# Attention steps of one kind in pairs: all full steps of a query tile first, its split steps after

## The chip, the cores and the metric

The kernel runs on one core of one Trainium2 chip. Its time is the device time of one execution in microseconds (us); of several runs the median is given. Shorter is better. A profiled execution is a run of its own, with the hardware profiler on, and it has its own time.

The engines are called as in the profile: PE is the matrix engine (PEld its weight loads), ACT the scalar engine, DVE the vector engine, POOL the general engine that also issues the gathers, SP the queue that issues plain transfers. PSUM is the memory into which PE writes.

## The reference, cut to what matters

A layer of graph attention and a mixture of experts, on 4096 rows of 512 numbers, all float32:

```
x = x + gnn(layernorm(x), adj)
x = x + ffn(layernorm(x))

gnn:  q, k, v = x @ Wq, x @ Wk, x @ Wv           # 8 heads of 64
      scores  = q @ k.T / 8 + 0.01*eye - 1e16*(1 - max(adj, eye))
      out     = softmax(scores) @ v @ Wo          # summed over heads
ffn:  2 of 8 experts a row, each gelu(x @ W1 + b1) @ W2 + b2, weighted
```

The adjacency matrix is sparse, and its first rows and columns are much denser than its last. A query attends only to the keys that its row of the adjacency matrix names.

## The kernel before, in words

Four stages follow each other: projections and lists of keys, attention, routing, experts. The change lies in the second.

**Lists and tiles.** The queries are cut into 32 tiles of 128. For a tile, the first stage makes a list of those keys that at least one of its queries needs, in three classes: needed only by the first 64 queries of the tile, needed by both halves, needed only by the last 64. `ROOM` (line 31) holds for each tile the room of the three classes in units of 128 keys, `(ta, tm, tb)`: (3, 22, 3) for the first tile, (6, 8, 6) for the second, (3, 2, 3) for the last eight.

**Steps.** A tile's work is a row of steps (lines 627 to 638). Each has a width of 128 keys by 128 queries:

- one step of kind `own`: the 128 keys of the tile's own rows, loaded by SP;
- `tm` steps of kind `both`, here called full steps: one gathered tile of 128 keys against all 128 queries;
- `ta` steps of kind `split`: two gathered tiles, one of keys for the first 64 queries and one of keys for the last 64.

There are 270 steps: 32 own, 115 full, 123 split. A gathered tile is 128 rows of 4640 bytes (keys, values and mask words), fetched by one indirect transfer from POOL (line 675); there are 115 + 2 x 123 = 361 of them.

**What a step does.** `turn` (line 694) transposes the gathered keys on PE (four transposes a key tile, line 701), ACT copies them out of PSUM (line 703), DVE unpacks the mask bits (line 713). `scores` (line 727) multiplies keys by queries on PE: a full or own step does it as 64 x 128 pieces of the array, 16 matmul records, a split step as 64 x 64 pieces, 64 records (line 738). ACT takes the exponential (line 745), DVE masks (line 751, or 749 for own). `values` (line 757) multiplies the result by the values, 32 records of 128 x 64 a step (line 766), and adds into the tile's output in PSUM from the first step to the last; the steps of a tile can stand in any order after the first.

**Duos and the order of the work.** Steps are taken in pairs, the duos (lines 642 to 645), which never cross a tile: with an odd number of steps a tile's last duo holds one. The order on every engine is the order in which this loop writes the instructions:

```
        duos = []
        for i in range(NT):
            own = [n for n, st in enumerate(steps) if st["i"] == i]
            duos += [own[k : k + 2] for k in range(0, len(own), 2)]
...
        while n < S or any(k >= n for k in later):
            duo(scores, n + 1)
            duo(values, n)
...
                issue(n + 1 + AHEAD)
            for job in later.pop(n, []):
                job()
            duo(turn, n + 3)
```

So one turn of the loop is: scores of the next duo, values of this one, issue of the gathers of the duo six ahead (`AHEAD` is 5, line 1005), whatever stands in `later`, and the transposes of the duo three ahead. What stands in `later` are a finished tile's end (transposes of line 797, output projection of line 805, residual) and, for each group of four tiles, routing for the experts (lines 831 to 1003: statistics, transposes of line 877, gate matmuls of line 886, ranks, scatters by POOL). These jobs hang on the number of the duo, not on its kinds.

**Buffers.** The pool `kvp` holds 20 key tiles (line 622), taken in turn; a gather waits until `values` has read the tile that was in its buffer. `ps_r` is three buffers of two PSUM banks (line 617), taken in turn by the scores, the transposes and the jobs. There are four buffers each of transposed keys and of exponentials.

Of the kernel before, what the change touches and what calls it, by code (L numbers as in the profile page):

```python
# [72 lines left out]
def fast(tc, dram, flag_d, x, adj, Wks, Wqs, Wvs, Wo, Wg, bg, W1, b1, W2, b2, out):  # L73
    with ExitStack() as ctx:
        _fast(ctx, tc, dram, flag_d, x, adj, Wks, Wqs, Wvs, Wo, Wg, bg, W1, b1, W2, b2, out)


def _fast(ctx, tc, dram, flag_d, x, adj, Wks, Wqs, Wvs, Wo, Wg, bg, W1, b1, W2, b2, out):
# [537 lines left out]
    with ExitStack() as s2:  # L616
# [11 lines left out]
        for i in range(NT):  # L628
            ta, tm, tb = ROOM[i]
            order = [("own", ())]  # L630
            for k in range(max(tm, ta)):
                if k < tm:
                    order.append(("both", (ta + k,)))
                if k < ta:
                    order.append(("split", (k, ta + tm + k)))
            for k, (kind, at) in enumerate(order):
                steps.append(dict(i=i, kind=kind, at=at, k=k, last=k == len(order) - 1,
                                  kv=[], wv=[], kT=[]))
# [1147 lines left out]
```

## Time and profile before

| | |
|---|---|
| median of 3 runs | 2134.53 us (2132.27 to 2135.46) |
| the profiled execution's own time | 2268.75 us |
| its span | 2267.0 us |
| PE busy | 2034.1 us, 90% of the span |
| DVE, ACT, POOL busy | 961.2, 799.3, 604.4 us |
| mean granted PE clock | 0.948 |
| attention in the profiled execution | first scores at 465.8 us, last values at 1605.5 us |
| gathers (line 675) | 361, 1.127 us each on POOL |
| PE instructions | 25404 matmul records, as many weight loads |

The profile is one execution. Its page gives the busy time of each engine, groups of equal instructions (count, busy time, mean length, idle time before them and what ended it), and transfers by queue. The trace behind it can be asked for who waited for whom, for the instructions in order of time, and for busy times by stretches. A wait that is put down to "issue" is one that no semaphore event in the trace ended. "PE" rows are matmul records, and matmuls overlap, so a mean length is longer than the time from one start to the next.

### The profile page before, as it was taken

How to read it: one execution, taken by the hardware profiler on the slowest of the kernel's cores; microseconds unless marked ns; L12 is line 12 of the kernel's file. 1: busy time of each engine (PE TensorE's matmuls, PEld its weight loads, DVE VectorE, ACT ScalarE, POOL GpSimd, SP SyncE). 2: the span in 40 equal slices, each digit the busy share in tenths (PEclk: the TensorE clock that was granted, in tenths of full speed). 3: DMA queues.
4: the chain of work that ended last, by engine and by line, in shares of the span. 5: the costliest groups of instructions: out<-in, count | busy, mean ns of one | idle time of the engine just before them, and what ended most of it. 6: DMA issues, size and time to landing. Idle time of an engine off the chain costs nothing. (4 is left out here: it accounts for less than half of the span.)

```text
span 2267.0 us, 59365 instructions
## 1 busy us (share of the span) xinstructions
PE 2034.1 (90%) x25404; PEld 1349.4 (60%) x25404; DVE 961.2 (42%) x2479; ACT 799.3 (35%) x1166; POOL 604.4 (27%) x712
## 2 busy tenths in 40 slices
PE   9999999989999889889797988979419999999997
PEld 4444444478777778777676876768314444444443
DVE  3665555435444445434444543545332332332322
ACT  3333333155445345344353543535102222222221
POOL 2000000144444434433444433342111112112111
PEclk9999999999999999889898998999759999999999
DMA  9878773487777677767677666675682333333332
GB/s 372 311 242 269 243 259 108 151 331 229 251 243 252 222 248 238 245 222 247 208 260 235 238 199 236 232 235 168 220 301 48 70 70 66 71 69 67 70 68 47
DMA packets 177522, 445.43 MB, mean 196 GB/s; under 512 B 23268, under 2 KB 39652, under 8 KB 176996
## 3 DMA queue, kind: packets, MB, share of 16 engines
q0 software_dynamic: 67360, 249.96, 36.5%
q1 hardware_dynamic: 82228, 141.61, 19.1%
q10 hardware_dynamic: 27664, 49.97, 6.1%
q8 instruction: 205, 3.36, 0.6%
q14 instruction: 65, 0.53, 0.1%
HBM read 367.53 MB, written 73.95 MB: 195 GB/s over the span
## 5 line engine op out<-in xcount | busy, mean ns | idle before, releaser
L675 POOL DMA_INDIRECT kv<-kv_d,idx x361 | 407.0, 1127 | 1026.8 <-issue 471.3
L738 PE MATMUL ps<-q,kT 64*64 64x64 f32 (+1 forms) x10224 | 362.4, 243 | 93.7 <-issue 78.9
L751 DVE SCALAR_TENSOR_TENSOR pr<-t,pr 128x1024 f32<-128x1024 uint16 x238 | 285.4, 1225 | 351.2 <-ACT pr L745 351.1
L738 PEld LDWEIGHTS ps<-q,kT 64*64 64x64 f32 (+1 forms) x10224 | 306.4, 152 | 147.6 <-issue 121.6
L703 ACT COPY kT<-pkT 128x512 f32<-128x512 f32 (+1 forms) x270 | 199.0, 783 | 369.9 <-PE pkT L701 250.0
L766 PE MATMUL o<-kv,pr 128*64 128x65 f32 x8640 | 309.4, 230 | 16.0 <-issue 15.6
L745 ACT ACTIVATE pr<-ps 128x1024 f32<-128x1024 f32 x270 | 271.8, 1025 | 124.9 <-PE ps L738 110.9
L766 PEld LDWEIGHTS o<-kv,pr 128*64 128x64 f32 x8640 | 284.8, 144 | 39.3 <-issue 24.8
L1181 PE MATMUL ph<-w,xT 128*128 x568 | 258.5, 598 | 0.7 <-ACT xT L1171 0.7
L1201 PE MATMUL py_e<-w,hT 128*128 x568 | 255.6, 593 | 0.9 <-DVE hT L1195 0.9
L1215 POOL DMA_INDIRECT out_dram<-y,r x71 | 110.8, 1561 | 474.7 <-ACT y L1214 469.8
L701 PE MATMUL pkT<-ident,kv 128*128 128x128 f32 x1572 | 204.7, 277 | 23.3 <-issue 18.8
L701 PEld LDWEIGHTS pkT<-ident,kv 128*128 128x128 f32 x1572 | 174.8, 142 | 48.5 <-issue 38.3
L1181 PEld LDWEIGHTS ph<-w,xT 128*128 128x128 f32 x568 | 103.5, 192 | 104.7 <-issue 103.5
L1201 PEld LDWEIGHTS py_e<-w,hT 128*128 128x128 f32 x568 | 102.5, 190 | 103.5 <-issue 102.3
L1186 DVE TENSOR_TENSOR h<-ph,bb 128x512 f32<-128x512 f32 x71 | 49.1, 692 | 212.8 <-PE ph L1181 209.8
L1213 DVE TENSOR_TENSOR y<-py_e,bb 128x512 f32<-128x512 f32 x71 | 49.1, 692 | 194.2 <-PE py_e L1201 194.2
L591 PE MATMUL pv<-wv,xT 128*128 128x512 f32 x256 | 131.3, 608 | 0.0
L591 PE MATMUL pk<-wk,xT 128*128 128x512 f32 x256 | 128.8, 614 | 0.7 <-ACT xT L389 0.7
L1187 ACT ACTIVATE h<-h 128x512 f32<-128x512 f32 x71 | 44.7, 629 | 233.1 <-DVE h L1186 233.1
L576 PE MATMUL pq<-xT,wq 128*128 128x512 f32 x256 | 125.9, 607 | 0.0
L805 PE MATMUL py<-wo,oT 128*128 128x512 f32 x256 | 121.7, 619 | 0.3 <-ACT pr L745 0.3
(248 smaller groups left out, 1727.2 us busy)
## 6 DMA issues: line engine op xcount, KB each, us to landing
adj<-in_adj_dram SPq DMA_DIRECT2D x64, 1024.0 KB
r<-xs_d SPq DMA_DIRECT2D x71, 258.0 KB
kv_d<-kvr ACTq DMA_DIRECT2D x32, 516.0 KB
kv<-kv_d SPq DMA_DIRECT2D x32, 516.0 KB
w<-in_L_ffn_W_dram ACTq DMA_DIRECT2D x16, 1024.0 KB
xt<-in_x_dram SPq DMA_DIRECT2D x32, 256.0 KB
q_d<-qT ACTq DMA_DIRECT2D x32, 256.0 KB
q<-q_d SPq DMA_DIRECT2D x32, 256.0 KB
```

Of the source, the lines that this page charges most:

```text
L576: nc.tensor.matmul(pq, w["q"][:, c, ts(p, P)], xTs[b][:, c, :], start=(c == 0), stop=(c == DC - 1),)
L591: nc.tensor.matmul(pk, xTs[b][:, c, ts(t, P)], w[n][:, c, :], start=(c == 0), stop=(c == DC - 1),)
L675: nc.gpsimd.indirect_dma_start(out=g, out_offset=None, in_=kv_d, in_offset=bass.IndirectOffsetOnAxis(ap=idx[i // GL][:, i % GL, a : a + 1] ...
L701: nc.tensor.transpose(pk[:, x * NP + p, :], g[:, ts(p, P)], ident)
L703: nc.scalar.copy(kT[:, : nk * NP], pk[:, : nk * NP])
L738: nc.tensor.matmul(ps[c : c + nk, r, p * P + x * nq : p * P + (x + 1) * nq], kT[r * KD : (r + 1) * KD, p, c : c + nk], q[r * KD : (r + 1) ...
L745: nc.scalar.activation(pr.rearrange("p h q -> p (h q)"), ps.rearrange("p r f -> p (r f)"), AF.Exp)
L751: nc.vector.scalar_tensor_tensor(pr, st["t"].unsqueeze(1).to_broadcast([P, H, P]), 0.0, pr, op0=ALU.is_gt, op1=ALU.mult,)
L766: nc.tensor.matmul(o[c * HALF : (c + 1) * HALF, h // NP, (h % NP) * VW : (h % NP + 1) * VW], pr[:, hd * NP + p, c * HALF : (c + 1) * HALF] ...
L805: nc.tensor.matmul(hold["py"], hold["oT"][:, c, :], wo[:, c, :], start=(c == 0), stop=(c == NP - 1),)
L1181: nc.tensor.matmul(ph, xTs[b][:, c, :], w1[:, bass.ds(es[b], 1), c, :], start=(c == 0), stop=(c == DC - 1),)
L1201: nc.tensor.matmul(py, hTs[b][:, c, :], w2[:, bass.ds(es[b], 1), c, :], start=(c == 0), stop=(c == HC - 1),)
```

## The change

Within a tile the order of the steps after `own` changes. Before, full and split steps alternate until one kind runs out; after, all full steps come first and then all split steps. Nothing else is edited.

```
         for i in range(NT):
             ta, tm, tb = ROOM[i]
             order = [("own", ())]
-            for k in range(max(tm, ta)):
-                if k < tm:
-                    order.append(("both", (ta + k,)))
-                if k < ta:
-                    order.append(("split", (k, ta + tm + k)))
+            order += [("both", (ta + k,)) for k in range(tm)]
+            order += [("split", (k, ta + tm + k)) for k in range(ta)]
             for k, (kind, at) in enumerate(order):
                 steps.append(dict(i=i, kind=kind, at=at, k=k, last=k == len(order) - 1,
                                   kv=[], wv=[], kT=[]))
```

As `own` and `both` do the same on PE (but for the source of the keys and the mask), the duos before and after are:

| duo | before | after |
|---|---|---|
| own + full | 32 | 32 |
| full + full | 9 | 32 |
| split + full (either order) | 64 | 19 |
| split + split | 21 | 43 |
| one split alone | 17 | 18 |
| one full alone | 1 | 0 |
| all | 144 | 144 |

A tile of (3, 3, 3), for example, goes from own+full, split+full, split+full, split to own+full, full+full, split+split, split.

## The prediction

> **What bounds the kernel now.** I read the page's slices first, then the waits of PE, then PE's instructions in order of time. Each digit of the slices is a busy share in tenths.
>
> ```profile
> PE   9999999989999889889797988979419999999997
> PEclk9999999999999999889898998999759999999999
> q8 instruction: 205, 3.36, 0.6%
> ```
>
> Slices 8 to 28 are attention: PE is nearly full there (1003.7 of 1130 us between 470 and 1600) while DVE has 530.7, ACT 520.1 and POOL 445.0. The chain that ended last shows only the last experts, so the waits must tell what PE lacks:
>
> ```profile
> PE ps L738 <- issue: 78.9, 149, 2.2
> PE pkT L701 <- issue: 18.8, 13, 4.8
> PE o L766 <- issue: 15.6, 27, 2.3
> PE ps L738 <- ACT kT L703: 4.3, 5, 2.0
> PE pkT L701 <- ACT kT L703: 4.2, 1, 4.2
> ```
>
> Columns: waiter, releaser, us in total, times, longest. Waits for another engine are a few us; "issue" makes 113 us. So attention is bound by PE's own stream: by its pace and by holes in it that no semaphore ended.
>
> The pace, in undisturbed duos (start, length, instruction; what counts is start to next start). Mixed:
>
> ```profile
> 741.33 1.47 PE L701 MATMUL pkT<-ident,kv 128*128 128x128 f32 x12
> 742.73 2.25 PE L738 MATMUL ps<-q,kT 64*64 64x64 f32 x80
> 744.91 2.09 PE L766 MATMUL o<-kv,pr 128*64 128x65 f32 x64
> ```
>
> Two split steps, and a hole after them:
>
> ```profile
> 838.17 1.04 PE L701 MATMUL pkT<-ident,kv 128*128 128x128 f32 x8
> 839.14 2.10 PE L738 MATMUL ps<-q,kT 64*64 64x64 f32 x128
> 841.17 2.09 PE L766 MATMUL o<-kv,pr 128*64 128x65 f32 x64
> 843.18 0.77 PE L701 MATMUL pkT<-ident,kv 128*128 128x128 f32 x5
> 846.51 0.55 PE L701 MATMUL pkT<-ident,kv 128*128 128x128 f32 x3 [2.56 <-issue]
> ```
>
> Two full steps:
>
> ```profile
> 525.78 2.06 PE L738 MATMUL ps<-q,kT 64*128 64x128 f32 x32
> 527.76 2.08 PE L766 MATMUL o<-kv,pr 128*64 128x65 f32 x64
> ```
>
> Scores take 2.18 us mixed, 2.03 split, 1.98 full. The hole lies among eight transposes whose inputs are there: PE had no instructions.
>
> **What the Trainium skill says.** "TensorEngine Tiling (Array Packing)", Key Properties: changing the tiling mode drains the array. The trace agrees: 0.15 to 0.20 us pass where the piece shape changes, 0.01 to 0.09 us inside a run. "Runtime: NRT & Kernel Launch", Instruction fetch mechanics: instructions come in 16 KiB blocks of 256 through a queue of the engine's own, and this is mostly hidden. The trace agrees on the blocks (queue 8: 205 packets, 16384 bytes each, for 51979 PE-side records). It does not agree on hidden: counting records against packets, 21 blocks in attention were used 1.25 to 1.55 us after their packet ended, the least there is, with PE standing still; these holes sum to 27 us. "DMA: Bandwidth & Descriptors": an engine goes round its queues by whole packets. An instruction block thus queues with gather packets, and in the trace it takes 3.3 to 8 us (5% and 95%) from when it seems to be asked for until use.
>
> **The change part by part.**
>
> *Mode changes, removed.* Mixed duos go from 64 to 19; 45 become 22 split and 23 full ones (the odd split step stays alone). A mixed duo's scores cost 2.18 against (2.03 + 1.98)/2 = 2.005 us: 0.175 saved. Transposes are linear (0.97 to 1.03 us for 8, 1.40 for 12, 1.84 for 16) and give back up to 0.02. So 45 x 0.155 to 45 x 0.175 is 7.0 to 7.9; I take **-7.5 us**. All else on PE is the same instructions.
>
> *Instructions in bunches, added.* A record has its weight load, so a mixed duo has 2 x (80 + 64 + 12) = 312 instructions, a split one 2 x (128 + 64 + 16) = 416, a full one 208. By matching packets with instruction counts, block k is asked for about 140 instructions into stretch k of 256 and must be there about 309 instructions later. At 5.6, 5.9 and 5.0 us a duo, 309 instructions last 5.6, 4.4 and 7.4 us. Jobs (lines 797, 805, 877, 886; some 175 us over 144 duos, few instructions) add 1.2 us a duo: 6.7, 5.3, 9.2 us. The block took 4.7, 5.5, 6.6 us (quartiles, split duos) and 3.7, 4.8, 6.1 (mixed). Setting each measured latency against these times gives a mean lateness a block of 0.92 to 1.56 us in split duos, 0.11 to 0.35 in mixed, 0 in full. Before: 45 x 312/256 = 55 blocks x 0.2 = 11 us. After: 22 x 416/256 = 36 blocks x 1.2 = 43 us. That is +32, too much: a late block slows PE and gives the next one time. At the profiled pace (split duos 9.8 us, mixed 9.1) the same sum gives 36 x 0.25 - 0 = +9, and there the trace bears it out: 7.5 us over 33 blocks of split duos, 0.23 each (mixed: 12.8 over 79, 0.16 each, which the sum misses). Lower end: 22 x 0.36 - 45 x 0.20 = -1 us, from those holes a duo as they stand. I take the middle of -1 and 32, **+16 us**.
>
> *Moved: gathers.* 361 before and after, issued by duo number as before. A gather keeps the 16 transfer engines for 1.77 us (packet times summed, over 361), so a split duo needs 7.1 us in 5.9 and a full one 3.5 in 5.0. The 20 buffers cover the difference: the tightest key tile landed 10.3 us before its transposes, the median 27. Counting tiles, the tile 20 back is never less than six duos away, before and after (40 and 49 gathers are at six). Cost 0; with that cover gone, 1.2 us for each of 22 split duos, +26.
>
> *Moved: other queues and engines.* SP's own tiles, queries and rows keep their duo numbers, and so do POOL's counters and scatters, which stand behind waiting gathers as before; nothing on PE waits for a scatter here. A split duo asks of ACT 2 x 1.01 + 2 x 1.03 = 4.1 us, of DVE 2 x 1.23 + 4 x 0.22 = 3.3, of POOL 4 x 1.24 = 5.0: all under PE's 5.9, which hides them. Where routing's two norms (0.81 each) fall on such a duo ACT comes level with PE; late next would be line 703 and with it a PSUM buffer, at most 1 us in each of 7 groups. I take 0, range 0 to +7.
>
> *Sum.* -7.5 + 16 = +8.5 us. In the profiled execution it is -7.5 + 9 = +1.5 on 2268.75. That execution is 134 us above the median, and attention must hold most of it: the stages before and after run at PE's pace. Many holes of line 738 are 0.6 us each with some six matmuls between them, away from block ends; they look like the profiler's own. Without them PE eats blocks faster, so I set the +8.5 against the median: **2143.0 us**.
>
> **The rivals.**
>
> 1. *Only the drains go* (ends faster). The place is the change of piece shape in line 738, the price 0.175 x 45. It decides if blocks take under about 4.4 us without the profiler. For it: the drains are certain, and the profiler may itself lengthen the fetch. Against: 7 of 33 blocks were late in split duos even at the slow pace. 2134.5 - 7.5 = 2127.0 us.
> 2. *The two cancel.* Latencies 15% shorter give 36 x 0.63 - 55 x 0.06 = 19, halved for the same reason 10: 2134.5 - 7.5 + 10 = 2137 us, and within 4 of no change over most of that neighbourhood.
> 3. *Gathers come too late.* 2134.5 - 7.5 + 26 + 8 = 2161 us. Against it: 10.3 us of slack, no wait for a gather on line 701.
> 4. *Holes of line 738 are real and fall with the pairing.* Holes over 0.35 us inside the scores make 1.28 us in a mixed duo, 0.59 in a split and 0 in a full one: 45 x 1.28 - 22 x 0.59 = 45 us, 2134.5 - 7.5 - 45 = 2082 us. Against it: the 134 us that only the profiled execution has.
> 5. *The pairs don't form.* Excluded: PE's order in the built program has the pairs of the table, with the same count of instructions.
>
> **How the numbers follow.** A measurement of this kernel tells 0.2%, 4.3 us, from no change. Forecast (slower by 4.3 to 22): 0.48. Rival 1: 0.27. Rival 2: 0.18. Rival 3: 0.04. Rival 4: 0.03. Slower is 0.48 + 0.04 = 0.52, faster 0.27 + 0.03 = 0.30, same 0.18. The likeliest case alone is 2139 to 2156. The range has to reach rival 1, whose own runs to -12: 2122. Above it takes in ACT's +7 and most of the +32: 2160. Left out are rivals 3 and 4 and the ends, under 2 in 10.
>
> **What would show it.** Right: scores of one kind at 2.0 us and 19 mixed duos at 2.18; more "issue" holes at block ends in split pairs, none in full ones; gathers still over 5 us early. Wrong: no more late blocks than 21, or PE waiting for gathers or for line 703.

## The result, and the profile after

The change makes the kernel slower: 2152.95 us against 2138.39 us, medians of 12 runs each, ratio 1.0069 (95% interval 1.0044 to 1.0095). That is +14.6 us; the forecast was +8.5.

Runs come in sets, each on one chip, and the kernel before took 2134 to 2138 us in some (the first sort; the result is of it) and 2261 to 2273 us in others (the second sort; the profile of 2268.75 us that the prediction was made from is of it). So before and after are compared here on traces of the first sort: the changed kernel's, of an execution of 2159.35 us, and one of the kernel before, run `b2`, of an execution of 2138.88 us.

From here on line numbers of the changed kernel are three lower than those of before (735 for 738, 763 for 766, 698 for 701). First PE's slices and granted clock, changed kernel:

```profile
PE   9999999989889988989999998889159999999997
PEclk9999999999999999999999999999579999999998
q8 instruction: 205, 3.36, 0.6%
```

PE is about as full as in the first profile, and its granted clock is steadier in attention, 0.97 in the mean against 0.94; this comes back below. Its waits, longest first, in the changed kernel:

```profile
PE o L763 <- issue: 55.1, 29, 3.9
PE ps L735 <- issue: 18.5, 14, 3.6
PE pkT L698 <- issue: 7.0, 6, 2.2
PE pkT L698 <- ACT kT L700: 5.8, 1, 5.8
```

and in the kernel before, run `b2`, the same view:

```profile
PE o L766 <- issue: 30.4, 21, 3.1
PE ps L738 <- issue: 17.0, 15, 3.3
PE pkT L701 <- issue: 10.8, 6, 3.4
PE pkT L701 <- ACT kT L703: 6.0, 1, 6.0
```

This is the loss in one line: waits without a releaser ("issue") in front of the values matmuls went from 30.4 to 55.1 us. No wait for ACT or DVE grew by more than 0.3 us in attention, and none for a gather appears. Where these holes lie is seen in PE's instructions in order of time, changed kernel, a split pair:

```profile
1060.14 1.84 PE L735 MATMUL ps<-q,kT 64*64 64x64 f32 x101 [0.56 <-issue]
1061.90 1.03 PE L763 MATMUL o<-kv,pr 128*64 128x65 f32 x27
1066.07 1.32 PE L763 MATMUL o<-kv,pr 128*64 128x65 f32 x37 [3.14 <-issue]
```

Within the 128 score matmuls of a split pair PE stops for 0.56 us; then it runs 101 of them and 27 of the values, and stands still for over 3 us. No semaphore ends either wait. Between the two holes lie 128 matmuls, which with their weight loads are 256 instructions, one block. A mixed and a full pair of the same kernel have none:

```profile
1076.43 2.06 PE L735 MATMUL ps<-q,kT 64*128 64x128 f32 x32
1078.41 1.15 PE L763 MATMUL o<-kv,pr 128*64 128x65 f32 x32
...
1081.39 2.25 PE L735 MATMUL ps<-q,kT 64*128 64x128 f32 x80
1083.58 1.03 PE L763 MATMUL o<-kv,pr 128*64 128x65 f32 x27
```

(The 32 records are own+full, which is a full pair to PE; its scores take 1.98 us from start to start, the mixed pair's 2.19.)

Now the count that the prediction made, on both traces. An instruction block is 256 of PE's instructions, fetched as one packet of queue 8. A hole of PE is put down to a late block where PE goes on at a block's end, 1.25 to 1.6 us after that block's packet ended. In the changed kernel there are 50, together 90.6 us; in the kernel before (`b2`) 42, together 67.0 us. That these are block ends does not rest on the time alone: picked by time only (1.2 to 1.66 us after a packet), there are 42 holes in `b2` and 52 in the changed kernel, and when PE's records are counted by 256, all 42 and 48 of the 52 stand at the same place, 193 or 194. By the pair whose scores open the turn of the loop:

| turn opened by | before: pairs, late us, us a pair | after: pairs, late us, us a pair |
|---|---|---|
| split + split | 21, 35.2, 1.68 | 43, 74.3, 1.73 |
| mixed | 64, 25.5, 0.40 | 19, 4.4, 0.23 |
| full + full, own + full | 41, 1.3, 0.03 | 64, 0.3, 0.00 |
| one split alone | 17, 5.0, 0.29 | 18, 11.6, 0.64 |

The price of a split pair is the same in both kernels, 1.7 us; only their number doubled. (The other two prices moved: mixed pairs got cheaper, lone split steps dearer.) Attention lasts 1016.4 us in `b2` and 1035.6 in the changed kernel, +19.2. Scores at their undisturbed pace (lower quartiles 2.18 mixed, 2.02 split, 1.98 full, 1.09 alone, times the number of each) give 282.7 us before and 274.6 after, -8.1. Late blocks give +23.6. That leaves +3.7 for all else; the granted clock stood at half for 58.1 us of attention instead of 49.0, which could make it up. The two executions are 20.5 us apart and the medians 14.6, so these parts are those of one pair of executions, and some us too large for the medians.

### The profile page after: what moved, and what is told of

It is laid out like the page before. It is cut to its first block, busy times and chain, and to the rows that moved or that the text cites. A ratio compares the mean times of both kernels' runs of the same rounds, so it can differ in the third digit from the quotient of the medians.

```text
span 2157.5 us, 59362 instructions
## 1 busy us (share of the span) xinstructions
PE 1962.9 (91%) x25404; PEld 1304.1 (60%) x25404; DVE 960.0 (44%) x2479; ACT 796.2 (37%) x1166; POOL 590.6 (27%) x712
## 5 line engine op out<-in xcount | busy, mean ns | idle before, releaser
L672 POOL DMA_INDIRECT kv<-kv_d,idx x361 | 388.3, 1076 | 939.1 <-issue 469.4
L763 PE MATMUL o<-kv,pr 128*64 128x65 f32 x8640 | 298.2, 226 | 55.1 <-issue 55.1
L735 PE MATMUL ps<-q,kT 64*64 64x64 f32 (+1 forms) x10224 | 297.1, 236 | 26.5 <-issue 18.5
L763 PEld LDWEIGHTS o<-kv,pr 128*64 128x64 f32 x8640 | 273.9, 140 | 73.5 <-issue 60.6
L735 PEld LDWEIGHTS ps<-q,kT 64*64 64x64 f32 (+1 forms) x10224 | 268.8, 148 | 55.0 <-issue 32.8
L742 ACT ACTIVATE pr<-ps 128x1024 f32<-128x1024 f32 x270 | 267.1, 1024 | 63.4 <-PE ps L735 59.6
L802 PE MATMUL py<-wo,oT 128*128 128x512 f32 x256 | 129.4, 651 | 0.3 <-ACT pr L742 0.3
```

Source lines behind the costliest of these rows:

```text
L672: nc.gpsimd.indirect_dma_start(out=g, out_offset=None, in_=kv_d, in_offset=bass.IndirectOffsetOnAxis(ap=idx[i // GL][:, i % GL, a : a + 1] ...
L735: nc.tensor.matmul(ps[c : c + nk, r, p * P + x * nq : p * P + (x + 1) * nq], kT[r * KD : (r + 1) * KD, p, c : c + nk], q[r * KD : (r + 1) ...
L742: nc.scalar.activation(pr.rearrange("p h q -> p (h q)"), ps.rearrange("p r f -> p (r f)"), AF.Exp)
L763: nc.tensor.matmul(o[c * HALF : (c + 1) * HALF, h // NP, (h % NP) * VW : (h % NP + 1) * VW], pr[:, hd * NP + p, c * HALF : (c + 1) * HALF] ...
L802: nc.tensor.matmul(hold["py"], hold["oT"][:, c, :], wo[:, c, :], start=(c == 0), stop=(c == NP - 1),)
```

## The experiments

Theory: **instruction blocks come late**, because a split pair's scores use 256 instructions in 2.0 us. Rivals: the loss lies in something else that was moved (gathers, ACT, jobs), or the load over several duos decides and not the single pair.

**The kernel before again** (`b0`, `b1`, `b2`), no edit.

> The kernel before, unchanged, for a second look at its profile. If the 0.6 us holes inside the scores of line 738 in the first profile belonged to that one profiled execution, they are gone here and the span is near 2138 us. Late instruction blocks (holes of PE at a block's end, used 1.25 to 1.6 us after their packet) were 27 us in 21 blocks in the slow profile. Theory (instruction blocks come late): at the faster pace there are more of them than 27 us, some 60 to 80 us, but clearly fewer than the 91 us in 50 blocks of the changed kernel. Rival (something else slows the changed kernel, the late blocks are as many in both): 85 to 95 us here too.

> The kernel before once more, for its trace in this set. If the set is of the sort near 2138 us: no holes of 0.55 to 0.7 us, late blocks 55 to 80 us, clearly under the changed kernel's. Rival (late blocks as many as after): within 8 us of it.

> The kernel before, for its trace; which sort of set this is shows in its span (near 2138 or near 2265 us). Near 2138: theory of late blocks says 60 to 75 us of late blocks, 15 to 28 under the changed kernel's 88 to 91 in its set, and few holes of 0.5 to 0.7 us; rival (the changed kernel loses by something else there) says within 8 us of the changed kernel's late blocks. Near 2265: 24 to 30 us of late blocks and over 80 short holes, as in the two traces of that sort.

`b0` took 2275.84 us and `b1` 2252.31, in sets where the kernel before stands at 2271.87 and 2261.16 us; late blocks 30.0 and 24.3 us. So the first profile was no outlier of the profiler: a whole sort of sets runs like that. `b1`'s waits show what is different there:

```profile
PE ps L738 <- issue: 73.6, 138, 3.0
PE o L766 <- issue: 15.4, 25, 1.7
PE pkT L701 <- issue: 15.3, 13, 3.4
```

Many short holes lie in front of the score matmuls: 88 of 0.55 to 0.7 us inside runs of matmuls, away from block ends. `b2` has 4, the changed kernel none in its first set.

The granted clock is different too, and much of the time goes there. It stood at half for 117.0 us of attention in `b1`, 148.0 in `b0` and 128.7 in the first profile, against 49.0 in `b2`. In `b1` PE starts 9.2 matmuls a us at half clock and 19.9 at full clock. First `b1`'s clock, then `b2`'s:

```profile
PEclk9999999999999999989898998999659999999999
PEclk9999999999999999999999999999579999999998
```

Holes and clock go together. In `b1` matmuls come in bursts 0.75 us apart at full clock (first two lines) and 1.4 us apart at half clock (last two):

```profile
706.50 0.29 PE L738 MATMUL ps<-q,kT 64*64 64x64 f32 x2 [0.40 <-issue]
707.25 0.37 PE L738 MATMUL ps<-q,kT 64*64 64x64 f32 x5 [0.46 <-issue]
...
1093.74 0.49 PE L738 MATMUL ps<-q,kT 64*64 64x64 f32 x4 [1.06 <-issue]
1095.16 0.48 PE L738 MATMUL ps<-q,kT 64*64 64x64 f32 x4 [0.93 <-issue]
```

In the traces of `b1`, `b2`, `after1` and the changed kernel, 48 of the 52 stretches at half clock within attention begin where PE had stood still for over 30% of the 3.4 us before, while only 11 to 17% of all such spells are like that. So standing still seems to bring the half clock on; no run tests it. Nor does any run tell the chip from the rest: the sets of `b0`, of `b1` and of `mixed` below, all of the second sort, ran on three chips and that of `b2` on a fourth.

`b2` gave the comparison above, 67.0 against 90.6 us, inside what the theory said (60 to 75, and 15 to 28 less than after); the rival's "within 8 us" is out.

**The changed kernel in the other sort of set** (`after1`), no edit.

> The changed kernel, unchanged, beside the others. Runs of the kernel before stood near 2138 us in one set and near 2272 in another, where the traces show 83 to 86 holes of 0.55 to 0.7 us inside runs of matmuls, which the changed kernel's trace at 2157.5 us has none of; so a ratio is good only within one set. If this set is of the first sort: ratio 1.004 to 1.010 and late blocks 80 to 100 us. If it is of the second sort: PE is slower and blocks have more time, late blocks 40 to 70 us, ratio 0.998 to 1.004. Rival (the loss does not hang on PE's pace): 1.007 in both sorts.

2246.26 against 2261.16 us, ratio 0.9936 (0.9916 to 0.9955): **the sign turns round.** Late blocks were 43.3 us, within the expectation; the ratio was outside it, on the good side. Between the traces of `b1` and `after1`, late blocks grew by 19 us (24.3 to 43.3), scores shrank by 8, and the other holes over 0.35 us inside runs by 13 (118.8 to 105.7); these make -2 of the -6.6 us between the two spans (2250.6 and 2244.0). The clock goes the same way: it stood at half for 99.6 us of attention, not 117.0. In the waits of `after1` the same shift is seen, score waits down, values waits up:

```profile
PE ps L735 <- issue: 61.5, 97, 4.6
PE o L763 <- issue: 37.8, 59, 3.0
PE pkT L698 <- issue: 14.8, 12, 4.7
```

So there almost the same extra lateness (+19 us, where it was +23.6) is bought back by drains, by fewer short holes and by less time at half clock. The last two differ between traces of one and the same program too (117.0 to 148.0 us at half clock before), so it is not shown that the order of steps brings them. Not all of the 14.9 us between the medians is placed by this.

**Split pairs and other pairs in turns** (`alt`, `alt1`, `alt2`): the same 43, 32 and 19 pairs, in another order within the tile.

```
-            order += [("both", (ta + k,)) for k in range(tm)]
-            order += [("split", (k, ta + tm + k)) for k in range(ta)]
+            full = [("both", (ta + k,)) for k in range(tm)]
+            split = [("split", (k, ta + tm + k)) for k in range(ta)]
+            rest = (full + split)[1:]
+            pairs = [rest[k : k + 2] for k in range(0, len(rest), 2)]
+            odd = [pairs.pop()] if len(rest) % 2 else []
+            heavy = [p for p in pairs if p[0][0] == "split"]
+            light = [p for p in pairs if p[0][0] == "both"]
+            order.append(full[0])
+            while heavy or light:
+                for kind in (heavy, light):
+                    if kind:
+                        order += kind.pop(0)
+            for p in odd:
+                order += p
```

> The same pairs as the changed kernel, 43 split, 32 full, 19 mixed, but within a tile split pairs and the other pairs take turns. Theory with bunching over several duos: instructions per us even out over two duos, late blocks fall by 10 to 25 us against the changed kernel's 91 us, the drains stay saved, time 2128 to 2143 us, so faster than the changed kernel and perhaps than the one before. Theory with bunching inside one duo (256 instructions of a split pair's scores in 2.0 us are enough): no change against the changed kernel, 2148 to 2158 us. Rival (jobs of a tile's end or routing fall on other duos): time moves either way by under 5 us with late blocks as they were.

> Split pairs and other pairs in turns, the same pairs as the changed kernel. In the set near 2272 us it was 0.3% faster than the kernel before with 53 us of late blocks against 30. Theory of bunching over several duos: late blocks 10 to 25 us below the changed kernel's in this set, time 0.2 to 0.8% below the changed kernel. Theory of the burst in one duo: as the changed kernel within 0.2%.

> Split pairs and other pairs in turns. In the set near 2261 us its late blocks were as many as the changed kernel's (42 against 43 us), so the burst inside one split pair seems to decide, not the load over several duos. Near 2138 that theory says 80 to 95 us of late blocks and 0.4 to 1.0% over the kernel before. If the load over several duos decides: 60 to 78 us and within 0.3% of the kernel before. In a set near 2265: ratio 0.996 to 1.002 once more.

In the set at 2134.0 us (`alt2`): ratio 1.0109 (1.0066 to 1.0151), late blocks 83.9 us in 47 blocks, 63.0 of them in split pairs. In the two other sets: 0.9971 (0.9958 to 0.9984) with 52.9 us, and 1.0000 (0.9984 to 1.0016) with 42.0 us. Evening out the instructions over two duos helped little, 83.9 against 90.6 us, and the time not at all. The waits of `alt2` look like the changed kernel's (lines 775 and 747 are values and scores of this longer kernel):

```profile
PE o L775 <- issue: 45.3, 29, 4.0
PE ps L747 <- issue: 16.9, 15, 2.6
```

This speaks against the load over two duos and for the burst inside one split pair. One thing neither theory had forecast: in its set `alt1` was 0.7% slower than the changed kernel (2261.35 against 2246.26 us) with as many late blocks; its clock stood at half for 146.6 us of attention, the changed kernel's for 99.6. `alt` beside `alt1`, the same program, also shows how far two sets of one sort can differ.

**A split pair's scores apart** (`spread`), from the changed kernel.

```
-            duo(scores, n + 1)
-            duo(values, n)
+            m = duos[n + 1] if n + 1 < S else []
+            apart = [steps[s]["kind"] for s in m] == ["split", "split"]
+            if apart:
+                scores(m[0])
+                duo(values, n)
+                scores(m[1])
+            else:
+                duo(scores, n + 1)
+                duo(values, n)
```

> The changed kernel, but around a split pair's scores the values of the duo before are put between the two steps' scores; 43 duos get one change of piece shape more, +6 to +8 us of drains. Theory that the burst inside one duo (256 instructions in 2.0 us) makes blocks late: late blocks fall by 15 us or more against the changed kernel in this set and the time falls by 5 to 15 us. Theory that the load over two or more duos decides (416 instructions a duo against a block's time): late blocks stay within 8 us, time rises by 3 to 10 us.

Late blocks fell from 43.3 us (`after1`, same set) to 26.6, as the burst inside one duo says. The time did not follow: 2304.19 us, ratio 1.0186 (1.0167 to 1.0205), 58 us more than the changed kernel there. New waits for ACT appeared, for the exponentials (`pr`) above all:

```profile
PE o L763 <- issue: 25.5, 60, 1.6
PE ps L735 <- ACT pr L742: 19.8, 9, 3.1
...
PE ps L735 <- ACT kT L700: 10.1, 5, 6.0
```

The edit moves more than the burst, so its time says nothing on the price of late blocks. Its block count fits the burst but does not prove it: a kernel that runs 58 us longer gives its blocks more time anyway, and in the second sort of set that alone went with fewer late blocks.

**Fewer gathers** (`before_half`, `after_half`, `after_half2`). These kernels leave out the second gather of every split step.

```
             st = steps[s]
+            if x == 1:
+                st["kv"].append(st["kv"][0])
+                st["wv"].append(st["wv"][0])
+                return
             g = kvp.tile([P, KVW], I32, tag="kv", name=f"kv_{s}_{x}")
```

> The kernel before with the same cut, 238 gathers instead of 361: a split step uses its first gathered tile for both halves of the queries. Theory: late blocks fall to under 15 us, time to 2065 to 2105 us, and it is 4 to 9 us slower than the changed kernel with the same cut. Rival (late blocks do not depend on transfers): time stays within 10 us of 2138.

> The changed kernel with 238 gathers instead of 361: a split step uses its first gathered tile for both halves of the queries, so its second half attends to the wrong keys; PE, ACT and DVE do the same instructions. Theory: an instruction block's time falls with the load on the transfer engines, late blocks fall from 91 us to under 30, time falls to 2060 to 2100 us, and this kernel is 4 to 9 us faster than the kernel before with the same cut, which is the drains. Rival (the loss has nothing to do with transfers): it stays 10 us or more slower than the kernel before with the same cut.

> The changed kernel with 238 gathers instead of 361 (a split step uses its first gathered tile for both halves of the queries), once more for the sort of this set. Near 2265 us: 31 us of late blocks against 43 without the cut, ratio 0.976 to 0.983. Near 2138: if the load of gathers is what makes blocks late, 30 to 55 us of late blocks instead of 91 and a ratio of 0.975 to 0.99; if it is the burst alone at any load, 75 us or more and a ratio over 1.0.

All three fell in sets of the second sort. With a third fewer gathers a block takes less from its asking to its use: median 4.5 us instead of 5.0 (`b1`) in the kernel before, 4.9 and 4.7 instead of 5.4 (`after1`) in the changed one. Late blocks fall to 10.0 us, and to 32.5 and 34.6. So transfers lengthen a block's way, but the 20 us between the two orders stays at this lower load too, which I had not expected. In time the two orders are level, 2220.48 and 2222.06 us (ratios 0.9774, 0.9758 to 0.9791, and 0.9791, 0.9763 to 0.9818; `after_half2` 0.9765, 0.9740 to 0.9789). The 4 to 9 us that I wanted for the saved drains did not come. Lateness less drains would even make the changed order some 14 us slower, so here too something else was bought back. Of the 51 us that the cut saves in the kernel before, 20 are late blocks. The short holes fell with it: matmul starts 0.55 to 0.7 us apart inside a run number 77, 76 and 82 in the three traces of before of this sort and 48 in `before_half`, 73 in `after1` and 29 and 26 in the two cut ones.

**As few split pairs as can be** (`mixed`), from the kernel before.

```
             for k in range(max(tm, ta)):
+                if k < ta:
+                    order.append(("split", (k, ta + tm + k)))
                 if k < tm:
                     order.append(("both", (ta + k,)))
-                if k < ta:
-                    order.append(("split", (k, ta + tm + k)))
```

> Steps alternate beginning with a split one, so own+split 32 and split+full 82 make 114 mixed pairs, with 1 split pair instead of 21 and 11 full ones. Theory: in the set near 2138 us late blocks cost 1.7 us a split pair and 0.4 a mixed one, so 2 + 46 + a few = 48 to 55 us against 67 for the kernel before, while 50 more mixed pairs cost 50 x 0.175 = 9 us of drains: ratio 0.994 to 0.999. In a set near 2265 us, where short holes fall on mixed pairs and blocks have time: ratio 1.003 to 1.010, late blocks 10 to 18 us. Rival (late blocks follow the total of instructions, not the pairing): 60 us or more near 2138, ratio 1.002 to 1.006 there.

The set was of the second sort (before 2273.30 us), and there the kernel took 2240.85 us, ratio 0.9852 (0.9829 to 0.9876): 1.5% faster, where I had expected it slower. Late blocks were 27.6 us, not 10 to 18, so no fewer than in the kernel before of this sort (30.0 and 24.3): a mixed pair is not cheap by its kind, it costs some 0.2 us here. Its waits:

```profile
PE ps L738 <- issue: 45.2, 107, 1.5
PE o L766 <- issue: 41.5, 64, 2.8
```

Other holes inside runs came to 100.6 us against 120.4 and 118.8 (`b0`, `b1`) although mixed pairs went up from 64 to 114: a mixed pair's scores hold 0.4 us of them here where they held 1.2. So my reading that the short holes belong to mixed pairs is refuted; of this gain 19 us can be placed by them. The clock stood at half for 105.9 us of attention, against 117.0 to 148.0 in the three traces of before, which partly counts the same holes; the rest is not placed. This is the best in that sort of set of all kernels that leave nothing out. In sets near 2138 us it was not run.

## Why the prediction was right, and where it was not

1. **Bound: PE's own stream.** Held in both sorts; every large wait of PE in attention, before and after, is one without a releaser. In the second sort the granted clock, which the prediction left out, takes a part of that stream.
2. **Drains, -7.5 us.** Held: the pace of scores gives -8.1 (2.18, 2.02 and 1.98 us a pair).
3. **Instructions in bunches, +16 us.** The mechanism held. It is shown by position (holes at block ends, most of them after a split pair's scores) and by count (`b2` against the changed kernel: twice the split pairs, at the same 1.7 us). `alt2` fits it (83.9 us, hardly changed by evening out over duos), and so does `spread`, with the reserve made there. The term was too small: +23.6 us, which is split pairs +39.1, mixed pairs -21.1, lone split steps +6.6 and full pairs -1.0. Two steps of the prediction failed. The lone split steps were not in the sum. And the lower end of -1 us, like the holes that were said to bear out the +9 at the profiled pace, rests on holes booked to the wrong pairs: by the pair whose scores open the turn, as in the table above, the 27 us of the first profile are 22.1 for its 21 split pairs and 3.8 for its 64 mixed ones, 1.05 and 0.06 us a pair. The same sum is then 22 x 1.05 less 45 x 0.06, about +20 and not -1 us, and `after1` did measure +19. The pairs that were counted cost 22 x 1.7 less 45 x 0.40 in the first sort, 19.4 us; that the middle of -1 and +32 came near it was luck.
4. **The sum against the profiled execution, +1.5 us, and against the median, +8.5.** Setting the sum against the median was right, but for another reason than given. "They look like the profiler's own" is wrong: `b2`, profiled too, ran in 2138.88 us with 4 such holes. They belong to one sort of set. And the +1.5 for that sort missed the sign: `after1` gave 0.9936. So that the forecast had the sign right is in part luck: nothing in it says in which sort of set the change would be timed.
5. **Gathers, 0.** Held for the wait: none of PE for a gather appears. The slack was less than I wrote: the tightest key tile landed 4.0 us before its transposes after the change (5.7 in `b2`, medians 24 and 23), under the 5 us that I had named as a sign; PE is faster in these sets than in the profile I read, which may be why.
6. **Other engines, 0 to +7.** Held at 0: PE's wait for ACT before line 698 is 5.8 us once, as it was (6.0).
7. **Rivals.** Rival 1 (faster by the drains) is out in the sets near 2138, since late blocks rose by 23.6 us, and rival 2 (the two cancel) is out there too. Rival 4, holes of line 738 that are real and fall with the pairing, I gave 0.03. In the other sort of set they are real, the scores' waits did fall, 73.6 to 61.5 us, and the kernel is faster there: I had the evidence in the profile and explained it away. But they do not hang on the pairing as rival 4 priced them: inside the scores of a split pair they make 0.3 us in `b1` and 1.0 in `after1`.

Open: what the short holes and the half clock are that go together in one sort of set, whether the chip decides, and why both shrink for two so different orders as the changed kernel's and `mixed`.

## What to carry to other kernels

When PE stands still and no semaphore ends the wait, count its instructions: small matmul pieces can use up an instruction block faster than the next one comes, and then the order of work matters, not only its amount. Before sorting like with like, set what it saves against what it bunches: here the change of piece shape saved 0.18 us a pair, and a pair of dense steps cost 1.7 us of late blocks. Whether an order with hardly any dense pairs beats the kernel before where blocks are late most was not run (`mixed` ran in the other sort of set only). Book a hole to the instructions that used up the block before it, not to those that it happens to stand among. And make sure that a profile is of the same sort of run as the times it is to explain.

## What the runs showed of the hardware that was not expected

- The same program differs by 6% between sets (2134 to 2138 and 2261 to 2273 us), with the same transfers and, at full clock, the same pace of undisturbed matmuls. The difference is in over 80 holes of 0.55 to 0.7 us inside dense runs of matmuls, a few records apart, in others beside them, and in 117.0 to 148.0 us of attention at half the granted clock instead of 49.0, where the same holes are twice as far apart. One change had ratios of 1.0069 and 0.9936 in the two.
- Instruction blocks cost 67 us of 1016 in the kernel before in the faster sort. A block seems to be asked for some 309 instructions ahead of its need (in `b2` and in the changed kernel no packet in attention started more than 301 records ahead) and took 4.7, 6.0 and 7.0 us (quartiles, `b2`). The Trainium skill, "Runtime: NRT & Kernel Launch", Instruction fetch mechanics, calls the cost of going from one block to the next mostly hidden; here the measurement decides, and 42 of some 165 blocks were not.
- A third fewer gathers shortened a block's way by only 0.5 to 0.7 us in the median, in the second sort of set.
